# Boundary copies of turned blocks: from ScalarE out of PSUM to GpSimd out of SBUF, with another order of the turns

## The chip, the cores and the metric

The kernel runs on one core of a Trainium2 chip. The core has five engines that the profile names: PE (TensorE, matmuls; PEld is its loading of weights), DVE (VectorE), ACT (ScalarE), POOL (GpSimd) and SP (SyncE, which only issues DMAs here). Each engine works through its own instructions in a fixed order and waits for others through semaphores. The metric is the device time of one execution in microseconds (us), lower is better. Data is float32 throughout.

## The reference

The input x is 4 images of 256 channels and 64 x 64 pixels. Layer 0 computes a 7x7 convolution with dilation 2 to 128 channels, a 1x1 convolution to 49 channels, and a softmax over these 49; the result is used as per-pixel weights of the 49 shifted copies of x:

```
k = conv(x, w1, padding 6, dilation 2) + b1          # 4 x 128 x 64 x 64
k = conv1x1(k, w2) + b2                              # 4 x  49 x 64 x 64
attn = softmax(k, axis=1)
y[b,c,h,w] = sum over u,v of xpad[b,c,h+2u,w+2v] * attn[b,7u+v,h,w]
```

Layer 1 whitens y: it takes the mean and the 64 x 64 covariance of each of the 4 groups of 64 channels over all pixels, finds an inverse square root of it by five Newton steps, applies it to the centred y, and scales and shifts each channel.

## The kernel before, in words

The two convolutions are folded into one from 256 to 49 channels, computed in a transformed domain (evaluations of rows and columns at a few points, products on PE, interpolation back). The matmuls of this are in `conv_bank` (line 599, tile `cv`), one step for each image and row point, in three banks. DVE makes their inputs (`col_ops`, tile `xh`, lines 347, 350 and 354, with ScalarE copies at 541 and 547) and interpolates their results (tiles `pv`, `zz`, `lgx`, the same helper lines). ScalarE brings the products out of PSUM (line 610).

Dilation 2 splits an image into four phases; two of them share a slot of x in SBUF. Attention works through 16 phases of columns and rows, n = 0 to 15, four for each image. For each n the logits go through `softmax`, `move_terms` copies the weights into a skewed layout (tile `zt`) and POOL's DMA queue writes them to a scratch in DRAM (tile `sd`, line 1093); `load_band` reads them back through SP's DMA queue as a banded matrix (tiles `band` and `bandz`). The weighted sum over shifts is then a matmul of blocks of x with bands.

For that, a block of 8 x 16 pixels has to stand on the partitions. `make_block` (line 1162) turns it: two PE transposes (line 1169), one for each 128 channels, into a PSUM tile `tp`, and a copy of 128 x 256 into the SBUF tile `xb` (line 1175). There are three PSUM buffers of `tp`, which are also used by `turn_y` and `softmax`, and four buffers of `xb`. The phase is cut into an upper and a lower half of rows; each half has four blocks, `PIECES` (line 1188), and a fifth piece ("z"), the rows of the other half that the shifts reach at the boundary. This fifth piece is put together from half blocks: when the block with t8 = 1 or 2 is turned, 64 of its 128 partitions are copied a second time, to the upper or lower 64 partitions of the tile `xbz` (line 1183). ScalarE makes these copies, out of PSUM, like those to `xb`; once the list `tail` is filled, after the last conv step, DVE makes both.

`weighted_sum(n, half, k)` (line 1194, matmuls at 1211) adds piece k to the sum of the half, k = 4 or k = 0 being the boundary piece: the upper half ends with it, the lower half begins with it. The upper half's boundary piece comes from blocks of the lower half (t8 = 2), so these must be turned before the upper half is complete. `store_y` (1231 and 1229) brings the sum out of PSUM and adds a pivot. `turn_y` turns the result y back, for `moments` (line 1263), which sums the covariance in PSUM (tile `sig`).

`first_half(n)` and `second_half(n)` write these calls down; PE keeps program order. `first_half(n)` also turns the last four blocks of y of the phase before (`turn(4)` to `turn(7)`, line 1242) where that is still open. On the other engines the order is chosen by a scheduler with a cost model that gives the copies a high priority. `gap` puts a half after every few conv steps: the halves of n = 0 to 9 lie between conv steps (190 to 561 us), those of 10 to 15 follow the last conv step (561 to 662 us). After that `whiten` and the output stage follow.

POOL has almost no arithmetic: memsets at the start, and one pair of small copies (line 1424). Its queue issues the DMAs of lines 147, 161, 1093 and 1281.

Of the kernel before, what the change touches and what calls it, by code (L numbers as in the profile page):

```python
# [32 lines left out]
def kernel(  # L33
# [29 lines left out]
    nc = tc.nc  # L63
    B, C, H, W = x.shape
# [33 lines left out]
    def pe(ins):  # L98
        return tc.keep_in_program_order(ins)
# [9 lines left out]
    def tp():  # L109
        return ps_tp.tile([P, 512], F32, tag="tp", name="tp")  # L110
# [72 lines left out]
    t = tp()  # L183
# [3 lines left out]
    t = tp()  # L187
# [5 lines left out]
    for k in range(2):  # L193
        t = ps_cv.tile([P, 512], F32, name=f"cv{k}")
# [53 lines left out]
    for k, c0 in enumerate(range(0, P, CB)):  # L248
        n = min(CB, P - c0)
        t = cv_buf[k % 2]  # L250
# [15 lines left out]
    for k0 in range(0, KT, TB):  # L266
        n = min(TB, KT - k0)
        t = tp()
# [848 lines left out]
    def load_band(n, half):  # L1117

        if (n, half) in loaded or n not in moved:
            return  # L1120
        loaded.add((n, half))
        D = sd[n % 2][:]
        base = lambda t, h: (
            h * HS + TR8 * t * RS + (ROW0[t] - TR8 * t + R) * WS + COLS[h][0] - h * TC + R
        )
        t0 = 2 * half
        for h in range(2):
            nc.sync.dma_start(
                band[:, t0 : t0 + 2, h].rearrange("p t r w -> p t (r w)"),
                bass.AP(  # L1130
                    tensor=D.tensor,
                    offset=D.offset + base(t0, h),
                    ap=[[LS - 1, P], [base(t0 + 1, h) - base(t0, h), 2], [1, TROWS * WS]],
                ),
            )
        e = CR * half + (R if half else 0)
        for h in range(2):
            c0, c1 = COLS[h]
            dma = nc.sync.dma_start(
                bandz[h * 64 : (h + 1) * 64, half, :, c0:c1],  # L1140
                bass.AP(
                    tensor=D.tensor,
                    offset=D.offset + h * HS + (HALF - CR * half) * RS + e * WS + c0 - h * TC + R,
                    ap=[[LS - 1, 64], [WS, R], [1, c1 - c0]],
                ),
            )
        if (n, half) == (4 * B - 1, 1):
            bring_back(dma)

    blocks = {}  # L1150

    tail = []

    def tile_of(t, cc, t8, h, pc):

        return halves(t)[:, cc, h, TR8 * t8 : TR8 * (t8 + 1), bass.ds(pc, TC, 2)]

    def where(n):

        return slots[n // 2], n % 2  # L1160

    def make_block(n, m):

        xt, pc = where(n)
        t8, h = m
        t = tp()
        for cc in range(NCC):
            pe(
                nc.tensor.transpose(  # L1169
                    t[:, cc * P : (cc + 1) * P], tile_of(xt, cc, t8, h, pc), ident  # L1170
                )
            )
        xb = bpool.tile([P, C], F32, tag="xb", name=f"xb_{n}_{t8}{h}", bufs=4)
        with tc.high_priority():
            (nc.vector.tensor_copy if tail else nc.scalar.copy)(xb, t[:, :C])  # L1175
        blocks[n, m] = xb
        if t8 in (1, 2):
            z = ("z", 2 - t8)
            if h == 0:
                blocks[n, z] = bpool.tile([P, C], F32, tag=f"xbz{t8}", name=f"xbz_{n}_{t8}")  # L1180
            i = slice(0, 64) if t8 == 2 else slice(64, P)
            with tc.high_priority():
                (nc.vector.tensor_copy if tail else nc.scalar.copy)(  # L1183
                    blocks[n, z][h * 64 : (h + 1) * 64], t[i, :C]
                )


    PIECES = (
        ((0, 0), (0, 1), (1, 0), (1, 1), ("z", 0)),
        (("z", 1), (2, 0), (2, 1), (3, 0), (3, 1)),  # L1190
    )
    y_ps = {}

    def weighted_sum(n, half, k):

        m = PIECES[half][k]
        if k == 0:
            y_ps[n, half] = ps_y.tile([P, NCC, HALF, SW], F32, tag="y", name=f"y_{n}_{half}")
        ps = y_ps[n, half]
        xb = blocks[n, m]  # L1200
        if m[0] == "z":
            q0, nq = (HALF - R, R) if half == 0 else (0, R)
            c0, c1 = 0, SW
            rhs = bandz[:, half].rearrange("p r w -> p (r w)")
        else:
            q0, nq = ROW0[m[0]] - HALF * half, TROWS
            c0, c1 = COLS[m[1]]
            rhs = band[:, m[0], m[1], :, : c1 - c0]
        for cc in range(NCC):
            pe(  # L1210
                nc.tensor.matmul(  # L1211
                    ps[:, cc, q0 : q0 + nq, c0:c1],
                    xb[:, cc * P : (cc + 1) * P],
                    rhs,
                    start=(k == 0),
                    stop=(k == len(PIECES[half]) - 1),
                    skip_group_check=True,
                )
            )

    def store_y(n, half):
        yt, pc = where(n)
        ps = y_ps.pop((n, half))
        for cc in range(NCC):
            o = halves(yt)[:, cc, :, half * HALF : (half + 1) * HALF, bass.ds(pc, TC, 2)]
            i = ps[:, cc].rearrange("p r (h c) -> p h r c", h=2)
            with tc.high_priority():
                if tail and cc:
                    nc.vector.tensor_scalar(o, i, pivot[:, cc : cc + 1], None, ALU.add)  # L1229
                else:  # L1230
                    last = nc.scalar.activation(o, i, AF.Identity, bias=pivot[:, cc : cc + 1])  # L1231
        return last
# [4 lines left out]
    def turn_y(n, i):  # L1237
        yt, pc = where(n)
        t = tp()
        for cc in range(NCC):  # L1240
            pe(
                nc.tensor.transpose(  # L1242
                    t[:, cc * P : (cc + 1) * P],
                    tile_of(yt, cc, i // 2, i % 2, pc),
                    ident,
                )
            )
        yb = ybs[n, i] = yt_buf[i % NY]
        with tc.high_priority():
            return nc.scalar.copy(  # L1250
                yb.rearrange("p a g c -> p (a g) c")[:, :, :GW],
                t[:, :C].rearrange("p (e c) -> p e c", c=GW),
            )

    def moments(n, half):


        for i in range(4 * half, 4 * half + 4):
            yb = ybs.pop((n, i))
            for cc in range(NCC):  # L1260
                for g in range(P // GW):
                    pe(
                        nc.tensor.matmul(  # L1263
                            sig[g * GW : (g + 1) * GW, cc],
                            yb[:, cc, g, :GW],
                            yb[:, cc, g],
                            start=(count[0] == 0 and cc == 0),
                            stop=(count[0] == 4 * B * NCH - 1),
                            skip_group_check=True,
                        )  # L1270
                    )
            count[0] += 1
# [3 lines left out]
    def move(k):  # L1276

        nxt_k = {0: 5, 1: 6, 2: 7}.get(k)
        if nxt_k is not None:
            spill[k] = dram.tile([P, NCC * SH * W], F32, name=f"spill{k}")  # L1280
            nc.gpsimd.dma_start(spill[k], slots[k].rearrange("p a r w -> p (a r w)"))
            load_x(k, nxt_k, nc.gpsimd)
# [14 lines left out]
    def first_half(n):  # L1297
        last = open_n.pop() if open_n else None

        def turn(i):  # L1300
            if last is not None:
                turn_y(last, i)

        for m in PIECES[0][:2]:
            if (n, m) not in blocks:
                make_block(n, m)
        turn(4)
        turn(5)
        weighted_sum(n, 0, 0)
        make_block(n, PIECES[0][2])  # L1310
        turn(6)
        weighted_sum(n, 0, 1)
        make_block(n, PIECES[0][3])
        turn(7)
        make_block(n, PIECES[1][1])
        weighted_sum(n, 0, 2)
        make_block(n, PIECES[1][2])
        weighted_sum(n, 0, 3)
        weighted_sum(n, 0, 4)
        move_terms(n + 1, store_y(n, 0))  # L1320
        half_done.add(n)
        load_band(n + 1, 0)
        if last is not None:
            moments(last, 1)
            if last % 2:
                move(last // 2)
        make_block(n, PIECES[1][3])
        make_block(n, PIECES[1][4])
# [228 lines left out]
    n = [0]  # L1557
# [97 lines left out]
```

## Time and profile before

| | us |
|---|---|
| median of 3 runs | 741.35 (739.52 to 743.1) |
| the profiled execution | 735.81 |
| its span, first to last instruction | 734.0 |
| PE busy | 684.0 (93%) |
| DVE busy | 598.0 (81%) |
| ACT busy | 328.8 (45%) |
| POOL busy | 133.2 (18%), nearly all of it issuing DMAs |
| the 40 ACT copies to `xbz` | 368 ns each (median) |
| the 24 DVE copies to `xbz` | 422 ns each (median) |
| the 82 ACT copies to `xb` | 373 ns each (median) |

The stages, read from the profile: weights and the first image's conv steps up to about 190 us; conv steps of the other images with the attention of n = 0 to 9 between them up to 561; the rest of the attention up to 662; whitening up to 677; the output stage to the end. A row of the timeline gives start and duration in us, engine, line and operation, the tiles as out<-in, the shapes and, in brackets, how long the engine was idle before it and what ended that. "Busy" of PE is modelled and includes matmuls that overlap.

### The profile page before, as it was taken

The page shows a single profiled execution, that of the slowest core. Times are in us where ns is not written, and L with a number is a line of the kernel's source. Part 1 is how long each engine was busy: PE and PEld are TensorE (multiplying, and loading weights), DVE is VectorE, ACT ScalarE, POOL GpSimd, SP SyncE. Part 2 cuts the span into 40 slices and gives each one's busy share as a digit, 9 for nine tenths or more (in the row PEclk, how much of TensorE's full clock was granted, in tenths as well). Part 3 has the DMA queues.
Part 4 walks back from the last instruction along what each step waited for, and adds up shares of the span by engine and source line. Part 5 has one row for each costly group of instructions (what it writes and reads, how often), then busy time and mean ns, then how long its engine had stood idle before and what let it go on. Part 6 is the DMA issues. An engine that isn't in the chain of part 4 may idle for free.

```text
span 734.0 us, 19103 instructions
## 1 busy us (share of the span) xinstructions
PE 684.0 (93%) x7728; PEld 539.1 (73%) x7728; DVE 598.0 (81%) x1291; ACT 328.8 (45%) x919; POOL 133.2 (18%) x194
## 2 busy tenths in 40 slices
PE   6999999999898999998999999998999689997996
PEld 1449543478898988897999989888998678885231
DVE  3799998995796899999886899899998885435575
ACT  1424320133654655675545445716546222332564
POOL 0002526663021020020220200200211322100000
PEclk9999999999999999999999999999999979997899
DMA  8923999973665582157645820452641535472687
GB/s 322 259 92 103 239 387 212 229 179 90 169 173 150 206 299 68 60 188 257 173 111 201 266 69 1 104 168 72 166 103 37 106 75 126 107 271 117 246 354 316
DMA packets 78337, 126.10 MB, mean 172 GB/s; under 512 B 36471, under 2 KB 58664, under 8 KB 77096
## 3 DMA queue, kind: packets, MB, share of 16 engines
q1 hardware_dynamic: 59912, 64.52, 26.9%
q0 software_dynamic: 12288, 42.08, 21.8%
q10 hardware_dynamic: 6048, 18.27, 8.0%
q8 instruction: 61, 1.00, 0.5%
q14 instruction: 28, 0.23, 0.1%
HBM read 78.78 MB, written 52.36 MB: 179 GB/s over the span
## 4 chain that ended last, share of the span: by engine, by line
PE 38%; DVE 27%; issue 9%; ACT 6%; DMA 4%; POOL 4%; ACTq 0%; SPq 0%; POOLq 0%; DVEq 0%
PE cv L599 15%; PE y L1211 7%; PE tp L1595 4%; DVE xh L354 3%; PE tp L1242 3%; DMA band<-sd 3%; DVE pv L354 3%; POOL ahead L147 3%; PE sig L1263 3%; DVE zz L354 2%; PE tp L1169 2%; DVE rb L347 2%; DVE rb L354 2%; ACT d L1017 1%; DVE pv L350 1%
## 5 line engine op out<-in xcount | busy, mean ns | idle before, releaser
L599 PE MATMUL cv<-xh,wr 128*49 128x128 f32 x4160 | 231.5, 273 | 3.5 <-ACT xh L547 3.3
L599 PEld LDWEIGHTS cv<-xh,wr 128*49 128x49 f32 x4160 | 226.3, 124 | 6.9 <-ACT xh L547 3.5
L1211 PE MATMUL y<-band,xb 128*128 128x209 f32 x512 | 113.4, 348 | 7.0 <-DMA band<-sd 5.9
L1093 POOL DMA_DIRECT2D sd<-zt x128 | 67.3, 532 | 234.1 <-ACT zt L1076 159.9
L1211 PEld LDWEIGHTS y<-band,xb 128*128 128x128 f32 x512 | 87.8, 195 | 8.9 <-DMA band<-sd 4.8
L610 ACT COPY pv<-cv 113x486 f32<-113x486 f32 (+2 forms) x60 | 26.1, 435 | 95.6 <-PE cv L599 90.5
L1250 ACT COPY yt<-tp 128x256 f32<-128x256 f32 x128 | 45.4, 378 | 50.3 <-PE tp L1242 49.2
L1242 PE MATMUL tp<-ident,slot 128*128 128x128 f32 x256 | 51.4, 298 | 9.0 <-ACT yt L1250 6.7
L354 DVE SCALAR_TENSOR_TENSOR pv<-pv 113x162 f32<-113x162 f32 x176 | 53.1, 322 | 3.3 <-ACT pv L610 2.6
L1242 PEld LDWEIGHTS tp<-ident,slot 128*128 128x128 f32 x256 | 41.1, 205 | 15.9 <-ACT yt L1250 7.8
L1169 PE MATMUL tp<-ident,slot 128*128 128x128 f32 x256 | 50.0, 300 | 2.7 <-DVE xbz L1183 1.4
L1231 ACT ACTIVATE slot<-y,pivot 128x512 f32<-128x512 f32 x52 | 36.1, 741 | 34.5 <-PE y L1211 34.4
L1169 PEld LDWEIGHTS tp<-ident,slot 128*128 128x128 f32 x256 | 40.9, 204 | 6.2 <-DVE xbz L1183 1.8
L147 POOL DMA_DIRECT2D slot<-in_x_dram x20 | 33.9, 1695 | 50.6 <-issue 46.2
L1076 ACT COPY zt<-d 32x112 f32<-32x112 f32 (+2 forms) x132 | 38.2, 290 | 7.3 <-DVE d L1035 5.4
L1263 PE MATMUL sig<-yt 128*64 128x65 f32 x1024 | 37.7, 228 | 0.0
L1263 PEld LDWEIGHTS sig<-yt 128*64 128x64 f32 x1024 | 33.2, 140 | 5.7 <-issue 4.3
L354 DVE SCALAR_TENSOR_TENSOR xh<-ct 128x512 f32<-128x512 f32 x40 | 26.7, 689 | 12.4 <-PE cv L599 12.3
L1017 ACT ACTIVATE d<-tp,mx 128x49 f32<-128x49 f32 x96 | 27.5, 337 | 19.8 <-DVE mx L1000 19.8
L764 PE MATMUL acc<-slot,tap 128*49 128x256 f32 (+7 forms) x224 | 34.8, 468 | 0.0
L1175 ACT COPY xb<-tp 128x256 f32<-128x256 f32 x82 | 28.5, 376 | 11.6 <-PE tp L1169 11.1
L1229 DVE TENSOR_SCALAR slot<-y,pivot 128x512 f32<-128x512 f32 x12 | 9.0, 751 | 27.2 <-ACT slot L1231 27.1
(239 smaller groups left out, 1117.3 us busy)
## 6 DMA issues: line engine op xcount, KB each, us to landing
out_dram<-out SPq DMA_DIRECT2D x32, 512.0 KB, 3.6
band<-sd SPq DMA_DIRECT2D x64, 242.0 KB, 3.3
slot<-in_x_dram POOLq DMA_DIRECT2D x20, 512.0 KB, 7.1
sd<-zt POOLq DMA_DIRECT2D x128, 77.0 KB, 3.1
wr<-gd ACTq DMA_DIRECT2D x14, 588.0 KB, 5.3
wr<-gd ACTq DMA_DIRECT2D x14, 490.0 KB, 4.3
ahead<-in_x_dram POOLq DMA_DIRECT2D x12, 512.0 KB, 7.3
spill<-slot POOLq DMA_DIRECT2D x3, 2048.0 KB, 7.2
```

What stands on the lines that cost most here:

```text
L147: queue.dma_start(o[:, cc, h], src[:, :, pr, h * SW : (h + 1) * SW])
L354: return in_turn(STT(o, a, f, b, ALU.mult, ALU.add))
L599: nc.tensor.matmul(o, wv[:, sc, sr, cc], xv[bc][:, h * NCC + cc], start=(j == 0), stop=(j == len(terms) - 1), skip_group_check=True,)
L1017: nc.scalar.activation(d[:, h, i], lt[i // NI][:, i % NI, h, :KT], AF.Exp, bias=mx[:, i, h : h + 1], accum_out=s[:, h, i : i + 1],)
L1076: ins = nc.scalar.copy(o, i)
L1093: nc.gpsimd.dma_start(bass.AP(tensor=D.tensor, offset=D.offset + h * HS + g * RS, ap=[[LS, TC], [CR * RS, NCH], [1, KS * WS]],), zt[p0 : p ...
L1169: nc.tensor.transpose(t[:, cc * P : (cc + 1) * P], tile_of(xt, cc, t8, h, pc), ident)
L1211: nc.tensor.matmul(ps[:, cc, q0 : q0 + nq, c0:c1], xb[:, cc * P : (cc + 1) * P], rhs, start=(k == 0), stop=(k == len(PIECES[half]) - 1), s ...
L1231: last = nc.scalar.activation(o, i, AF.Identity, bias=pivot[:, cc : cc + 1])
L1242: nc.tensor.transpose(t[:, cc * P : (cc + 1) * P], tile_of(yt, cc, i // 2, i % 2, pc), ident,)
L1250: return nc.scalar.copy(yb.rearrange("p a g c -> p (a g) c")[:, :, :GW], t[:, :C].rearrange("p (e c) -> p e c", c=GW),)
L1263: nc.tensor.matmul(sig[g * GW : (g + 1) * GW, cc], yb[:, cc, g, :GW], yb[:, cc, g], start=(count[0] == 0 and cc == 0), stop=(count[0] == 4 ...
```

## The change

Outside the tail, the copy of the 64 boundary partitions is no longer made by ScalarE out of PSUM but by GpSimd, out of the SBUF block `xb` that ScalarE has just written. It therefore waits for the `xb` copy, and the PSUM buffer has one reader less. In `first_half` the second block of the upper quarter row is turned before `turn(6)` and the second sum, the first block of the lower half before `turn(7)`, and the second one before the third sum instead of before the fourth. The order applies to all 16 phases, the engine only to those before the tail.

```
             i = slice(0, 64) if t8 == 2 else slice(64, P)
             with tc.high_priority():
-                (nc.vector.tensor_copy if tail else nc.scalar.copy)(
-                    blocks[n, z][h * 64 : (h + 1) * 64], t[i, :C]
-                )
+                if tail:
+                    nc.vector.tensor_copy(blocks[n, z][h * 64 : (h + 1) * 64], t[i, :C])
+                else:
+                    nc.gpsimd.tensor_copy(blocks[n, z][h * 64 : (h + 1) * 64], xb[i])
...
         turn(5)
         weighted_sum(n, 0, 0)
         make_block(n, PIECES[0][2])
+        make_block(n, PIECES[0][3])
         turn(6)
         weighted_sum(n, 0, 1)
-        make_block(n, PIECES[0][3])
+        make_block(n, PIECES[1][1])
         turn(7)
-        make_block(n, PIECES[1][1])
+        make_block(n, PIECES[1][2])
         weighted_sum(n, 0, 2)
-        make_block(n, PIECES[1][2])
         weighted_sum(n, 0, 3)
         weighted_sum(n, 0, 4)
```

## The prediction

> **What bounds the kernel now.** I read the page first, for the engines' shares, then busy time by stretches, then the tile that the change is about, then the order of time in one of the places it touches.
>
> ```profile
> span 734.0 us, 19103 instructions
> PE 684.0 (93%) x7728; PEld 539.1 (73%) x7728; DVE 598.0 (81%) x1291; ACT 328.8 (45%) x919; POOL 133.2 (18%) x194
> ```
>
> PE is the bound on average, with 50 us idle in all. The stretches (us from the start; then PE, PEld, DVE, ACT, POOL busy) say more:
>
> ```profile
> 223.00:232.00 9.00, 7.14 (x70) 6.13 (x67) 8.93 (x16) 6.65 (x18) 0.30 (x1) 1.00 0.60 192
> ...
> 442.00:449.00 7.00, 6.80 (x71) 6.29 (x69) 6.93 (x6) 5.53 (x15) 0.00 (x0) 1.00 0.00 0
> ...
> 470.00:502.00 32.00, 28.50 (x520) 28.05 (x517) 30.98 (x68) 10.76 (x49) 4.05 (x8) 1.00 0.52 143
> ...
> 540.00:548.00 8.00, 7.80 (x80) 6.98 (x78) 7.69 (x15) 6.32 (x17) 0.00 (x0) 1.00 0.13 34
> ```
>
> 223 to 232, 442 to 449 and 540 to 548 hold the first halves of n = 1, 7 and 9. DVE has no gap in them and POOL does nothing. From 470 to 502 DVE, not PE, is the bound. The boundary tile, and who waits for the ScalarE copies of it:
>
> ```profile
> L1183 ACT COPY xbz<-tp x40: 363/368/374, 192.7 to 545.1; 64x256 f32<-64x256 f32 x40
> L1183 DVE COPY xbz<-tp x24: 406/422/428, 564.0 to 652.8; 64x256 f32<-64x256 f32 x24
> ```
>
> and from the list of waits (us in total, times, longest):
>
> ```profile
> PE y L1211 <- ACT xbz L1183: 5.5, 8, 1.5
> ```
>
> So the change touches 40 copies, four in each of ten first halves (n = 0 to 9); 24 stay on DVE. The end of the half of n = 9, PE and ScalarE rows, then DVE:
>
> ```profile
> 543.50 0.87 PE L1211 MATMUL y<-band,xb 128*128 128x209 f32 x4
> 544.21 0.39 PE L1169 MATMUL tp<-ident,slot 128*128 128x128 f32 x2
> 544.44 0.87 PE L1211 MATMUL y<-band,xb 128*128 128x209 f32 x4
> 545.51 0.69 PE L1211 MATMUL y<-bandz,xbz 128*128 128x96 f32 x4 [0.20 <-ACT xbz L1183]
> ```
>
> ```profile
> 544.71 0.38 ACT L1175 COPY xb<-tp 128x256 f32<-128x256 f32 x1
> 545.10 0.36 ACT L1183 COPY xbz<-tp 64x256 f32<-64x256 f32 x1
> ```
>
> ```profile
> 543.67 0.76 DVE L350 TENSOR_TENSOR zz<-zz 113x576 f32<-113x576 f32 x1
> 544.47 0.76 DVE L347 TENSOR_TENSOR zz<-zz 113x576 f32<-113x576 f32 x1
> ```
>
> The last block is turned at 544.21, one sum (0.7 us) covers its two ScalarE copies, and the boundary sum starts 0.20 late. The same wait in n = 0 to 8 is 0.30, 0.78, 1.50, 0.71, 0, 0.99, 0.25, 0.20, 0.87: 5.8 us with n = 9. At n = 1 the third block also waits 1.09 for a PSUM buffer that a boundary copy holds. Lastly the place that resets PE, and the only copy POOL makes:
>
> ```profile
> 497.44 1.81 PE L599 MATMUL cv<-xh,wr 128*49 128x128 f32 x29 [3.27 <-ACT xh L547]
> ```
>
> ```profile
> L1424 POOL COPY swap<-ident 128x64 f32<-128x64 f32 x2 | 0.4, 236 | 27.8 <-DVE lgx L354 27.8
> ...
> L295 POOL MEMSET zeros<- 128x256 f32 x1 | 0.3, 311 | 0.0
> ```
>
> At 497.44 PE has waited 3.27 us; the row names ScalarE, but DVE's last two writes of xh end at 497.33 and 497.94, so DVE was late.
>
> **The sum's base.** The profiled execution took 735.81 (span 734.0 and 1.81 around it); the median of the runs is 741.35, 5.54 more. I sum against 735.81 and add 5.54.
>
> **Part 1a, ScalarE loses 40 copies.** 40 x 0.39 start to start = 15.6 us of an engine busy 45%; it counts only where PE waits. A PSUM buffer comes free one copy (0.39) sooner, which removes the 1.09 at n = 1.
>
> **Part 1b, the order in a half.** Today the second block of the upper quarter is turned after the second sum and the last block just before the fourth. Now the last block is turned before the third sum, with two sums (1.43 us) ahead of the boundary sum. At n = 9 its transposes come 0.7 earlier, its ScalarE copy ends about 4.15 us after the half's start (540.22) and the boundary sum is due at 5.09. Instructions and sums stay the same in number; no DMA is moved.
>
> **Part 1c, a POOL copy alone.** No row has 64x256. From the copy of 64 elements (236 ns) and the memsets' slope ((311-205)/128 = 0.83 ns an element), 192 more elements make 395 ns. If what the copy takes beyond a 64-element memset (236-145 = 91 ns) also grows by the element, it is 670. I take 0.50, between, because only one copy row exists; ends 0.40 and 0.67. Ahead of it I put 0.15 (DVE's lgx ends 563.62, POOL's swap starts 563.77), behind it 0.1. If nothing else is in its way the last copy ends at 4.15+0.15+0.50+0.1 = 4.9, inside 5.09. That cover is 0.2 us thin.
>
> **Part 1d, a POOL copy beside DVE.** In the ten halves DVE is busy 82 of 87 us with 178 instructions, nearly all with two SBUF inputs, and the new copies read SBUF too. The only POOL copy of this trace ran when DVE had no such instruction, so no row tells whether they go side by side. Bounds: none of it (below), or POOL and DVE taking turns, each waiting for the other's whole instruction. The gain needs complete independence, since the cover is 0.2 and DVE has no gap, so I take turns as the likelier. In turns four copies wait for half an instruction and then for three whole ones, of a mean length L read from the stretch (busy by count). The first copy is ready 2.1 us after the half's start (n = 5, 7, 8 and 9 alike), so the boundary sum waits 2.1+0.15+4x0.50+3.5L+0.1-5.05 = 3.5L-0.7. By stretch: n = 1 (L 0.56) 1.26, n = 3 (0.47) 0.95, n = 5 (0.49) 1.0, n = 7 (1.16) 3.4, n = 8 (0.36) 0.56, n = 9 (0.51) 1.1. The halves without turned outputs, from their own starts: n = 2 1.8, n = 6 1.4. At n = 0 and 4 PE waits for the band DMA at the second sum; two copies are done by then, which leaves 0.7 and 0. DVE loses 4x0.5 = 2.0 us a half. Behind the waiting boundary sum PE has the moments, two block turns and the next conv bank queued, and ScalarE's store of y waits for it.
>
> [...]
>
> **What reaches the end, in turns.** PE delay, after minus before: n = 0 +0.4; n = 1 1.26-0.78-1.09 = -0.6; n = 2 +0.3 (the conv bank at 271.42 had its input 1.70 before, and DVE's 2.0 takes that too); n = 3 +0.2; n = 4 and 5 0; n = 8 -0.3. n = 6 and 7 delay PE by 4.3, of which the 3.27 at 497 swallows most, but DVE is full from 412 to 497 and comes 8x0.5 = 4.0 later: +4.0. Elsewhere the conv's inputs lie 4 to 19 us ahead of PE, so DVE's loss is hidden by that lead; without it each half would cost 2.0. After n = 9 DVE runs without a gap to its first tail copy at 563.54, which PE needs: +2.0 (PE's own 0.9 lies inside). Sum +6.0.
>
> **Part 2, the tail.** Six halves keep DVE copies: waits of 0.2 to 0.4 at the boundary sum (2.1 in all) and 1.42 at one block. The eight copies of a half are 8x0.42 = 3.4 us of DVE in a row, so the new order starts the last pair only some 0.3 earlier: I take -1.5, between -3.5 (all gone) and +1.4 (a turned output waiting for a DVE-held buffer costs what that block's wait did).
>
> **POOL's queue.** Copies share it with DMA issues of 0.53 each in eights (4.3). Those end at 223.30 and 373.73, before the copies of n = 1 and 5 are ready (225.4, 374.5); one load is issued at 342.24 inside n = 4, worth 0.57. The boundary copies for the second half's first sum are due 7 us later or more, and the block buffers they read are reused only after the boundary sum: no cost, unless POOL falls behind by more than that sum's wait.
>
> **Forecast:** 735.81+6.0-1.5 = 740.3, plus 5.54: **746**. With copies of 0.40 the sum is +2.6-1.5, 742.5; with 0.67 it is +11.9-1.5, 751.8. With the tail's ends the forecast's own range is 740 to 755.
>
> **Rivals.** (1) *Side by side, faster.* No interference, copies of 0.5: 5.8+1.09 of waits go, less 0.45 (n = 6 and 7, swallowed at 497), and 1.5 of the tail: -7.9, **733**. For it: POOL is idle in all ten halves. Against: the cover of 0.2 and DVE without gaps. It decides if a copy stays under 0.7 us beside DVE. (2) *POOL gets no turn while DVE has work queued.* At n = 9 DVE has no gap for 10 us; one half of 10 and two of 3 more make +16: **757** or more. Against: it needs the next DVE instruction always to win. (3) *Copies behind DMA issues*: a set of eight landing ahead of a last copy costs 4.3; two sets, beside the case (1): **742**. Against: the times above. (4) *It does nothing*: the removed waits reappear behind other ScalarE work (0.66 us xh copies stand before the last copy in n = 5 and 8), **741**.
>
> **Chances.** Turns 0.53 (slower 0.38, within 0.5% 0.12, faster 0.03); side by side 0.28 (faster 0.26, same 0.02); no turn 0.10; DMA issues 0.04 (same); nothing 0.05 (same 0.03, slower 0.02). Half a per cent, 3.7 us, is about what a measurement tells from no change. Faster 0.29, same 0.21, slower 0.50. The range runs from just below the first rival, 731, to the second, 757.
>
> **What would show it.** Turns: POOL copies of 0.4 to 0.7 that start 0.5 to 2 us after their ScalarE copy, boundary sums waiting about 1 us for POOL (n = 7 most), the wait at 497 near 7 us, DVE rows longer in the ten halves. Side by side: those sums start without a wait and DVE's means stay. What would make me wrong: a copy that is much longer than 0.67, or the order of ScalarE and DVE work shifting in the softmax of the last batch (580 to 594, where PE waits 5.9 us for reasons outside the change).

## The result and the profile after

The changed kernel takes 768.74 us (median; 768.54 to 769.98), the kernel before, run beside it, 740.43. The ratio is 1.0385 [1.036, 1.0409]: slower by 28 us, where 746 was forecast and 757 was the end of the range. The profiled execution took 768.57, its span is 766.8 (before 734.0).

The page of the changed kernel: the span, the engines, and two of the costliest groups (busy time and mean ns of one, then the idle time ahead of them and what ended it):

```profile
span 766.8 us, 19122 instructions
PE 693.2 (90%) x7728; PEld 549.1 (72%) x7728; DVE 601.2 (78%) x1291; ACT 314.2 (41%) x879; POOL 192.8 (25%) x234
...
L1186 POOL COPY xbz<-xb 64x256 f32<-64x256 f32 x40 | 59.7, 1493 | 135.4 <-ACT xb L1175 133.9
...
L1212 PE MATMUL y<-bandz,xbz 128*128 128x96 f32 x128 | 22.0, 300 | 35.1 <-POOL xbz L1186 35.1
```

PE's idle time went from 50.0 to 73.6 us, its busy time from 684.0 to 693.2 for the same 7728 matmuls. The two add up to the 32.8 by which the span grew. (The medians differ by 28.3: the profiled execution of the kernel before, 735.81, lies 4.6 under the median there.) The list of waits (us in total, times, longest) has what ended the idle time:

```profile
PE y L1212 <- POOL xbz L1186: 35.1, 9, 11.2
...
PE cv L599 <- ACT xh L547: 1.9, 1, 1.9
```

The boundary sums wait 35.1 us where they waited 5.5; all other idle time of PE together fell by 6.0. The answer for the boundary tile shows why (ns least, median and most, first and last start):

```profile
L1186 POOL COPY xbz<-xb x40: 396/744/12550, 192.8 to 580.7; 64x256 f32<-64x256 f32 x40
```

One copy takes 0.40 us at best, 0.74 in the median and 12.55 at worst. The 40 together are busy for 59.7 us, where 40 x 0.40 would be 16; the other 44 us GpSimd stood inside its copies. The worst one belongs to the first half of n = 8. Its rows of the timeline, POOL, then PE, then DVE from the moment the copy is released (the DVE rows are cut to the first and the last few):

```profile
527.83 12.55 POOL L1186 COPY xbz<-xb 64x256 f32<-64x256 f32 x1 [29.14 <-ACT xb L1175]
```

```profile
529.02 1.58 PE L1212 MATMUL y<-band,xb 128*128 128x209 f32 x8
541.80 1.17 PE L1212 MATMUL y<-bandz,xbz 128*128 128x96 f32 x4 [11.20 <-POOL xbz L1186]
```

```profile
527.80 0.32 DVE L354 SCALAR_TENSOR_TENSOR pv<-pv 113x162 f32<-113x162 f32 x1
528.04 0.32 DVE L347 TENSOR_TENSOR pv<-pv 113x162 f32<-113x162 f32 x1
528.28 0.56 DVE L350 TENSOR_TENSOR pv<-pv 113x162 f32<-113x162 f32 x2
...
535.49 2.36 DVE L354 SCALAR_TENSOR_TENSOR rb<-slot 128x1024 f32<-128x1024 f32 x2
537.76 2.36 DVE L354 SCALAR_TENSOR_TENSOR rb<-rb,slot 128x1024 f32<-128x1024 f32 x2
548.91 0.69 DVE L354 SCALAR_TENSOR_TENSOR xh<-ct 128x512 f32<-128x512 f32 x1 [8.79 <-PE cv L599]
```

DVE runs its queue without a gap: each row starts some 0.08 us before the one ahead of it has ended (535.49 + 2.36 = 537.85, the next at 537.76). It ends at 540.12, and the copy ends 0.26 later, at 540.38; the other three copies of the half then take 0.40 each. The last row tells why DVE stopped: its next instruction needs a product of PE, and PE is waiting for the copy. GpSimd got its turn when DVE had run out of work.

The five copies beside which three or more DVE instructions ended, worked out from the trace's records, with the wait of that half's boundary sum:

```
half   copy starts   copy takes   DVE instructions that ended beside it   DVE then stops for   sum waits
n = 8     527.83       12.55                    27                             8.79             11.20
n = 4     346.46        9.71                    21                             8.99              4.53
n = 1     225.50        4.55                     7                             0.035             4.57
n = 2     271.14        3.00                     5                             0.035             3.82
n = 3     306.12        2.49                     3                             4.63              1.39
```

All five end 0.26 to 0.27 us after a DVE instruction with a gap behind it. A gap of 0.035 us is what the records show where a DVE instruction reads the result of the one just before. Where DVE does such a chain (tile `zz`, n = 2, 6 and 9), one copy gets in after each instruction, and takes 0.58 to 0.83 (0.40 where it comes just at a gap).

The sums behind such a wait are slower as well: the boundary sum's four matmuls take 1.17 after the four longest waits (4.53, 4.57, 4.79 and 11.20 us), at a granted clock of 0.50, and 0.69 after the other five (0.53 to 3.82), at 1.00. The granted clock is 0.95 in the stretch of the halves (190 to 600 us) where it was 1.00 (190 to 562 before), and 0.955 over the whole span against 0.977. That fits the 9.2 us more of PE's busy time.

### The profile page after: what moved, and what is told of

The parts are those of the page before. It is cut to its first block, busy times and chain, and to the rows that moved or that the text cites. A ratio compares the mean times of both kernels' runs of the same rounds, so it can differ in the third digit from the quotient of the medians.

```text
span 766.8 us, 19122 instructions
## 1 busy us (share of the span) xinstructions
PE 693.2 (90%) x7728; PEld 549.1 (72%) x7728; DVE 601.2 (78%) x1291; ACT 314.2 (41%) x879; POOL 192.8 (25%) x234
## 4 chain that ended last, share of the span: by engine, by line
PE 51%; DVE 15%; issue 8%; POOL 7%; ACT 4%; DMA 3%; SPq 0%; ACTq 0%; POOLq 0%; DVEq 0%
PE cv L599 20%; PE y L1212 10%; PE sig L1264 4%; PE tp L1596 4%; POOL xbz L1186 4%; PE tp L1243 4%; PE tp L1169 3%; PE cv L764 3%; POOL ahead L147 2%; DMA band<-sd 2%; DVE xh L354 2%; DVE d L1035 2%; PE apply L1612 1%; PE cv L1612 1%; DVE zz L354 1%
## 5 line engine op out<-in xcount | busy, mean ns | idle before, releaser
L599 PE MATMUL cv<-xh,wr 128*49 128x128 f32 x4160 | 235.3, 276 | 1.9 <-ACT xh L547 1.9
L599 PEld LDWEIGHTS cv<-xh,wr 128*49 128x49 f32 x4160 | 230.3, 126 | 5.9 <-ACT xh L547 2.1
L1212 PE MATMUL y<-band,xb 128*128 128x209 f32 x512 | 110.5, 348 | 5.8 <-DMA band<-sd 5.6
L1186 POOL COPY xbz<-xb 64x256 f32<-64x256 f32 x40 | 59.7, 1493 | 135.4 <-ACT xb L1175 133.9
L1212 PE MATMUL y<-bandz,xbz 128*128 128x96 f32 x128 | 22.0, 300 | 35.1 <-POOL xbz L1186 35.1
L1243 PEld LDWEIGHTS tp<-ident,slot 128*128 128x128 f32 x256 | 41.4, 204 | 9.6 <-issue 3.6
L1169 PEld LDWEIGHTS tp<-ident,slot 128*128 128x128 f32 x256 | 39.0, 206 | 12.5 <-issue 8.5
L1212 PEld LDWEIGHTS y<-bandz,xbz 128*128 128x128 f32 x128 | 19.4, 213 | 38.6 <-POOL xbz L1186 38.6
L1264 PE MATMUL sig<-yt 128*64 128x65 f32 x1024 | 40.7, 238 | 0.0
L1264 PEld LDWEIGHTS sig<-yt 128*64 128x64 f32 x1024 | 36.0, 150 | 6.1 <-issue 4.9
```

The source lines that it names most:

```text
L599: nc.tensor.matmul(o, wv[:, sc, sr, cc], xv[bc][:, h * NCC + cc], start=(j == 0), stop=(j == len(terms) - 1), skip_group_check=True,)
L1169: nc.tensor.transpose(t[:, cc * P : (cc + 1) * P], tile_of(xt, cc, t8, h, pc), ident)
L1186: nc.gpsimd.tensor_copy(blocks[n, z][h * 64 : (h + 1) * 64], xb[i])
L1212: nc.tensor.matmul(ps[:, cc, q0 : q0 + nq, c0:c1], xb[:, cc * P : (cc + 1) * P], rhs, start=(k == 0), stop=(k == len(PIECES[half]) - 1), s ...
L1243: nc.tensor.transpose(t[:, cc * P : (cc + 1) * P], tile_of(yt, cc, i // 2, i % 2, pc), ident,)
L1264: nc.tensor.matmul(sig[g * GW : (g + 1) * GW, cc], yb[:, cc, g, :GW], yb[:, cc, g], start=(count[0] == 0 and cc == 0), stop=(count[0] == 4 ...
```

## The experiments

The theory after the result: GpSimd's read of SBUF is kept out by DVE for whole runs of instructions, and the boundary sums wait for that. The rivals: the new order costs the time; the copy's size or GpSimd's slowness costs it; GpSimd's writes are in the way; ScalarE did something useful before. All edits are made to the changed kernel, but for the last three, which are made to the order alone.

| kernel | us | ratio to before |
|---|---|---|
| changed kernel | 768.74 | 1.0385 [1.036, 1.0409] |
| order alone, ScalarE copies | 730.40 | 0.9869 [0.9836, 0.9901] |
| GpSimd alone, order as before | 775.89 | 1.0485 [1.0432, 1.0538] |
| 16 of 256 columns | 767.87 | 1.0377 [1.0325, 1.0429] |
| GpSimd writes, doesn't read | 731.72 | 0.9888 [0.9839, 0.9938] |
| DVE waits for each copy | 765.90 | 1.0359 [1.0316, 1.0402] |
| half of the copies on GpSimd | 739.51 | 1.0006 [0.9983, 1.0028] |
| DVE copies | 760.71 | 1.0291 [1.0222, 1.036] |

### The two parts apart

The order alone:

```diff
-                    nc.gpsimd.tensor_copy(blocks[n, z][h * 64 : (h + 1) * 64], xb[i])
+                    nc.scalar.copy(blocks[n, z][h * 64 : (h + 1) * 64], t[i, :C])
```

> Only the new order; the boundary copies stay on ScalarE out of PSUM. Theory (GpSimd's copies get no turn while DVE's two-input instructions follow one another): without GpSimd the loss is gone, 733 to 741 us, and the boundary sums of the ten halves wait under 3 us in all (5.8 before). Rival (the order itself costs, through PSUM buffers and queues): 750 us or more.

GpSimd alone, with the calls of `first_half` in the order of the kernel before:

```diff
         make_block(n, PIECES[0][2])
-        make_block(n, PIECES[0][3])
         turn(6)
         weighted_sum(n, 0, 1)
-        make_block(n, PIECES[1][1])
+        make_block(n, PIECES[0][3])
         turn(7)
-        make_block(n, PIECES[1][2])
+        make_block(n, PIECES[1][1])
         weighted_sum(n, 0, 2)
+        make_block(n, PIECES[1][2])
         weighted_sum(n, 0, 3)
```

> Only the engine: GpSimd copies out of SBUF, the order of before. Theory: the last copy becomes ready 0.7 us nearer to the boundary sum, so each of ten halves may wait 0.7 us more: 765 to 780 us, sums waiting for GpSimd 33 to 45 us. Rival (the order costs): about 745 us.

Measured: 730.40 and 775.89. The order alone is faster than both kernels and a little better than expected. In its list of waits the 5.5 us of the boundary sums are down to this:

```profile
PE y L1211 <- ACT xbz L1183: 0.8, 2, 0.6
```

GpSimd alone has the long waits too, 31.0 us where 33 to 45 were expected:

```profile
PE y L1212 <- POOL xbz L1186: 31.0, 8, 11.2
```

So the whole loss is GpSimd's and the order gains 10 us. The changed kernel is 38 us above the order alone. Between these two profiles the boundary waits differ by 35.1 - 0.8 = 34.3 us; the idle time of PE as a whole by 28.2 (73.6 against 45.4), its busy time by 10.2 (693.2 against 683.0, at a granted clock of 0.955 against 0.979), which add up to the 38.4 between the spans. Between the profiles of the kernel before and of the order alone it is 5.6 (734.0 and 728.4), not 10: the granted clock of the executions is 0.968 to 0.977 before and 0.972 to 0.981 with the order alone, and whether the order is the cause of that difference stays open.

### What of the copy is held up

The copy cut to 16 columns. A memset of the whole half block comes ahead of it, so 240 of 256 channels of the boundary pieces are zeros:

```diff
-                    nc.gpsimd.tensor_copy(blocks[n, z][h * 64 : (h + 1) * 64], xb[i])
+                    zb = blocks[n, z][h * 64 : (h + 1) * 64]
+                    nc.gpsimd.memset(zb, 0.0)
+                    nc.gpsimd.tensor_copy(zb[:, :16], xb[i, :16])
```

> As the changed kernel, but GpSimd copies 16 of the 256 columns (the other columns of the boundary block are zeros from an earlier GpSimd memset, so the boundary sums are not those of the reference). Theory: what costs is the wait for a turn, not the copying; 755 to 770 us, the longest copy still over 5 us, waits for GpSimd 25 us or more. Rival (GpSimd is slow at copying 64x256): a sixteenth of the data, so 745 us or less and no copy over 1.5 us.

No reading at all; the boundary pieces before the tail are zeros:

```diff
-                    nc.gpsimd.tensor_copy(blocks[n, z][h * 64 : (h + 1) * 64], xb[i])
+                    nc.gpsimd.memset(blocks[n, z][h * 64 : (h + 1) * 64], 0.0)
```

> As the changed kernel, but GpSimd fills the boundary half blocks with zeros instead of copying (no read, and no wait for the block; the boundary sums are left without their data). Theory: only an instruction that reads SBUF is held up by DVE; 730 to 739 us, no fill over 0.6 us. Rival (DVE keeps GpSimd from SBUF altogether, or GpSimd's queue with its DMA issues is what is late): fills of several us, 750 us or more.

Measured: 767.87 and 731.72. The groups of the page, first the kernel with 16 columns, then the one that only writes:

```profile
L1188 POOL COPY xbz<-xb 64x16 f32<-64x16 f32 x40 | 49.6, 1240 | 120.1 <-ACT xb L1175 118.6
```

```profile
L1186 POOL MEMSET xbz<- 64x256 f32 x40 | 12.2, 307 | 218.9 <-PE y L1212 213.8 <-PE acc L764 4.3
```

A copy of a sixteenth of the size, 0.19 us where it is undisturbed, still takes 1.24 us in the mean and 12.35 at most, and the kernel gains nothing by it: the size made no difference here. A memset of the full size takes 0.307 us wherever it lies, about what the 128 x 256 memset took in the profile before (0.3 us), and 37 of the 38 us are gone. (The memset needs no block to be turned, so it can start earlier than a copy; but 31 of the 40 run wholly beside DVE instructions with two operands, at 0.305 to 0.312 us.) What DVE keeps out here is GpSimd's reading of SBUF (copies of up to 12.55 us), not its writing.

### Three ways around it

Here DVE is made to wait for each copy by a one-column copy that reads the boundary block:

```diff
                     nc.gpsimd.tensor_copy(blocks[n, z][h * 64 : (h + 1) * 64], xb[i])
+                    probe = work.tile([P, 1], F32, tag="probe", name=f"probe_{n}_{t8}{h}", bufs=2)
+                    nc.vector.tensor_copy(
+                        probe[h * 64 : (h + 1) * 64], blocks[n, z][h * 64 : (h + 1) * 64, :1]
+                    )
```

> As the changed kernel, but behind each GpSimd copy DVE gets a copy of one column of the boundary block, so that it has to stop until GpSimd has finished. Theory (GpSimd's copy needs a moment in which DVE's two-input instructions do not follow one another): the stop gives it that moment; the longest copy falls from 12.6 to under 3 us, sums waiting for GpSimd from 35 to under 12 us, time 735 to 750 us, which is what the prediction had for taking turns. Rival (the wait is GpSimd's own, whatever DVE does): 765 us or more.

Measured: 765.90, a miss; by its time alone the rival (765 or more) would fit. The scheduler put the readers late in DVE's order, so copies still took up to 9.6 us. But the long ones of three halves, followed in the records, ended just where a reader stopped DVE. In the half of n = 8, POOL (two copies in one row), then DVE:

```profile
529.47 6.93 POOL L1186 COPY xbz<-xb 64x256 f32<-64x256 f32 x2 [29.07 <-ACT xb L1175]
```

```profile
534.78 0.32 DVE L350 TENSOR_TENSOR pv<-pv 113x162 f32<-113x162 f32 x1
535.39 0.14 DVE L1188 COPY probe<-xbz 64x1 f32<-64x1 f32 x1 [0.29 <-POOL xbz L1186]
```

Eighteen instructions after the release DVE comes to the first reader. Its queue was not empty at 535.10, it was only made to wait, and the first copy, which had stood since 529.47, ended at 535.36. So GpSimd's wait is not its own: in these halves it ended where DVE stopped. That the remedy failed says nothing against the cause; it names what is needed, a stop of DVE at the right place.

Only half of the copies on GpSimd, those of t8 = 1, which are due later, for the second half's first sum:

```diff
+                elif t8 == 2:
+                    nc.scalar.copy(blocks[n, z][h * 64 : (h + 1) * 64], t[i, :C])
                 else:
                     nc.gpsimd.tensor_copy(blocks[n, z][h * 64 : (h + 1) * 64], xb[i])
```

> New order; GpSimd copies only the two half blocks that the second half needs (t8 = 1), ScalarE the two that end the first half. Theory: the late copies are no longer in front of the boundary sum, so PE does not wait for GpSimd there; but the block buffer that a late copy reads is needed again for the third block after it, which in the two longest cases (10 and 12 us) holds up ScalarE: 731 to 742 us. Rival (any GpSimd copy costs what its wait costs, about 0.9 us each): 748 us or more.

Measured: 739.51, no change from before and 9 worse than the order alone. The boundary sums wait for GpSimd no more (one waits 1.6 for ScalarE), but the copies still stand (up to 16.03 us) and hold the blocks that they read:

```profile
ACT xb L1175 <- POOL xbz L1188: 16.0, 5, 11.1
...
PE cv L599 <- ACT pv L615: 9.1, 1, 9.1
```

ScalarE waits for one of the four `xb` buffers, and PE, once, for ScalarE's work queued behind that. A copy that nobody needs for 7 us still costs, if it stands longer than its source is free to stay.

DVE makes all boundary copies, as in the tail:

```diff
-                if tail:
+                if True:
```

> New order; DVE makes all boundary copies, out of PSUM. Each half gives DVE 4 x 0.42 us more, as much as GpSimd's turns were to cost it in the prediction. If DVE's lead over PE hides that except at the wait at 497 us and at the tail, as the prediction had it, the time lies 3 to 7 us above the new order alone: 733 to 738 us. If DVE is the bound in most stretches: 745 us or more.

Measured: 760.71, a miss by 22. The copies queue in DVE's order, and until they are done they hold the PSUM buffers that the next transposes need:

```profile
PE tp L1169 <- DVE xbz L1184: 20.0, 6, 7.1
...
PE tp L1243 <- DVE xbz L1184: 10.9, 4, 4.1
```

Of the three engines tried for these copies ScalarE serves best: 730.40 against 760.71 with DVE and 768.74 with GpSimd.

### When DVE gives a turn

The last three kernels add groups behind the end of the work: DVE instructions in a row, with GpSimd copies of 64 x 256 released beside them by a DVE copy (line 1658, 1666 or 1664; in two groups of the last kernel by ScalarE), so their total times say nothing. The first one, ten instructions of 128 x 512 of five kinds, one after another in program order:

```diff
...
+    for j, kind in enumerate((two, one_psum, psum_only, one, reduce)):
+        s, g = qs[j % 2][:, :256], qg[j % 2][:, :256]
+        keep(nc.vector.tensor_copy(s, chain[0]))
+        keep(nc.gpsimd.tensor_copy(g[0:64], s[64:128]))
+        keep(nc.gpsimd.tensor_copy(g[64:128], s[0:64]))
+        for k in range(10):
+            keep(kind(k))
+        chain[0] = g
```

> The kernel with the new order alone, and behind its end five groups: DVE makes a block, GpSimd copies its halves (two copies of 64x256) while DVE runs ten instructions of one kind on 128x512: sum of two SBUF operands; sum of one SBUF and one PSUM operand; copy out of PSUM; multiple of one SBUF operand; reduction of one SBUF operand. Theory: GpSimd's first copy ends under 0.8 us after its block with all kinds that read SBUF once, and only after the tenth instruction (6 us or more) with two SBUF operands. Rival (any busy DVE keeps GpSimd out): late in all five. Rival (GpSimd is late for its own reasons): late in none. The additions lengthen the kernel by some 30 us, which says nothing.

Measured, the first GpSimd copy of each group, in the order: two operands in SBUF, one in SBUF and one in PSUM, a copy out of PSUM, one SBUF operand times a constant, a reduction:

```profile
724.59 0.73 POOL L1659 COPY qg<-qs 64x256 f32<-64x256 f32 x1 [102.68 <-DMA out_dram<-out]
...
731.15 0.40 POOL L1659 COPY qg<-qs 64x256 f32<-64x256 f32 x1 [5.02 <-DVE qs L1658]
...
737.33 0.40 POOL L1659 COPY qg<-qs 64x256 f32<-64x256 f32 x1 [5.34 <-DVE qs L1658]
...
743.51 3.55 POOL L1659 COPY qg<-qs 64x256 f32<-64x256 f32 x1 [5.33 <-DVE qs L1658]
...
747.91 0.40 POOL L1659 COPY qg<-qs 64x256 f32<-64x256 f32 x1 [0.39 <-DVE qs L1658]
```

Beside additions with an operand in PSUM, copies out of PSUM and reductions GpSimd's copies took 0.40 us, as long as the shortest in the kernel. The products with a constant, which ran at 0.34 us each, half the time of the others, kept it out to the end of all ten. But the additions of two SBUF operands, the kernel's main kind, let it in by turns here. Both are against what was expected of them. So the kind alone doesn't say why it stands for 27 instructions in the kernel. The second one asks whether multiply-and-add, length or the moment makes the difference:

```diff
...
+    for j, (kind, lead) in enumerate(
+        ((stt, 0), (tt, 4), (mixed, 4), (small, 4), (long, 2), (in_place, 4))
+    ):
+        s, g = qs[j % 2][:, :256], qg[j % 2][:, :256]
+        for k in range(lead):
+            keep(kind(k))
+        keep(nc.vector.tensor_copy(s, chain[0]))
...
```

> ScalarE's copies out of PSUM with the new order, and behind the end of the kernel's work six groups, each with a DVE copy that releases two dependent-free GpSimd copies of 64x256 and then ten DVE instructions of one kind, all with two SBUF operands: multiply-and-add of 128x512; addition of 128x512 with four more of them ahead of the release; the two kinds in turn; addition of 113x162; multiply-and-add of 128x1024; addition of 128x512 in place, each on the result of the one before. The total time says nothing (25 to 35 us of added work). Theory, that the kind of instruction decides: the additions let a GpSimd copy in after one instruction, as the ten additions of before did (copies of 0.73 and 0.75), and the multiply-and-adds keep it out for several, so the first copy beside them takes over 2 us (128x512) and over 3 us (128x1024). Rival, that it is the length or the moment and not the kind: then the copies beside the multiply-and-adds of 128x512 take 0.7 to 0.8 as well, and those beside the short or the long ones differ. Only the chain in place has a pause after every instruction, in which both expect a turn.

Measured, the first copy of the first, second and fourth group:

```profile
726.19 0.73 POOL L1667 COPY qg<-qs 64x256 f32<-64x256 f32 x1 [103.06 <-DVE qs L1666]
...
735.16 8.62 POOL L1667 COPY qg<-qs 64x256 f32<-64x256 f32 x1 [7.43 <-DVE qs L1666]
...
752.18 2.57 POOL L1667 COPY qg<-qs 64x256 f32<-64x256 f32 x1 [5.98 <-DVE qs L1666]
```

My theory on the kind fell. Multiply-and-adds gave turns (0.73). The same additions of 128 x 512 that gave turns before now kept a copy out for 8.62 us: ten of them and the four instructions of the next group, until DVE itself had to wait. What changed is what ran ahead of the release: memsets and a copy there, here four additions, behind the ten multiply-and-adds of the first group without a gap. The short ones, with four ahead in the same way, kept it out for all ten (2.57). In the third and sixth group DVE had a pause just ahead, or one after each instruction, and the copies took 0.80. The long ones gave turns as well (1.33), but all ten wrote the same tile, so each had to wait for the one before; that group doesn't test length.

The third one varies what lies ahead of the release. Additions of 128 x 512 in all groups, none, or four of them, ahead of the release, and ten behind it (in the last group those behind it have one operand in PSUM):

```diff
...
+    for kind, lead, how, copies in (
+        (tt, 0, "DVE", 6),
+        (tt, 0, "late", 2),
+        (tt, 4, "PSUM", 2),
+        (tt, 4, "ACT", 2),
+        (tt, 4, "DVE", 2),
+        (one_psum, 4, "DVE", 2),
+    ):
...
```

> ScalarE's copies out of PSUM with the new order, and behind the end six groups of ten DVE additions of 128x512 with two SBUF operands (the last group: one operand in PSUM), none on the result of the one just before it, with GpSimd copies of 64x256 released beside them. Every group begins with a pause of DVE. (1) released right after the pause, six copies; (2) released after the pause by a chain of six ScalarE copies, some 2 us later; (3) to (5) released after four additions without a pause, by a DVE copy out of PSUM, by a ScalarE copy, by a DVE copy out of SBUF; (6) like (5), the additions behind it with one operand in PSUM. The total time says nothing. [...] Rival, that the DVE copy out of SBUF right before decides and not the pause: (2), (3) and (4) show turns as (1) does, and (5) alone a long copy.

The theory that this tests: DVE gives turns only shortly after a pause (copies of 0.73 to 0.8 us in group 1), and a copy released later stands until DVE stops (4 us or more in groups 2 to 5); in group 6 a copy takes about 0.4.

Measured, one row for each group (the copies of a group in one row):

```profile
725.72 4.75 POOL L1671 COPY qg<-qs 64x256 f32<-64x256 f32 x6 [102.86 <-DVE qs L1664]
736.00 3.95 POOL L1671 COPY qg<-qs 64x256 f32<-64x256 f32 x2 [5.54 <-ACT qs L1668]
743.15 1.53 POOL L1671 COPY qg<-qs 64x256 f32<-64x256 f32 x2 [3.20 <-DVE qs L1664]
752.60 6.18 POOL L1671 COPY qg<-qs 64x256 f32<-64x256 f32 x2 [7.92 <-ACT qs L1662]
761.85 6.60 POOL L1671 COPY qg<-qs 64x256 f32<-64x256 f32 x2 [3.07 <-DVE qs L1664]
771.52 0.85 POOL L1671 COPY qg<-qs 64x256 f32<-64x256 f32 x2 [3.07 <-DVE qs L1664]
```

Groups 1, 4, 5 and 6 went as the theory had it, and group 2 too but for the size (its first copy took 3.50, where 4 or more were expected). The copy released in the first addition after other work (here memsets) got its turn, and so did the five behind it: 4.75 / 6 = 0.79 each. The copies released nearly three microseconds into the run of additions, or after four or five of them, stood until DVE stopped, whether ScalarE or a DVE copy from SBUF released them (3.95, 6.18 and 6.60 for the two copies of a group). Group 3 corrects the theory: turns came without a pause. A DVE instruction that reads PSUM, put between the fourth and the fifth addition, was enough for turns (0.77 each). So what sets these groups apart is whether DVE had been reading two SBUF operands for several instructions without a break when the copy was released. The kernel has one copy that doesn't fit: at n = 0 one was released at 196.14, while the fourth such instruction of 113 x 162 without a gap was running, and had its turn after that one and the next (0.60).

## Why the prediction was wrong

**Parts 1a and 1b, right in size; the credit went to the wrong part.** The first rival priced the change without interference at -7.9, 733. With nothing read by GpSimd it is 731.72, and the order with ScalarE's copies reaches 730.40. So freeing ScalarE of 40 copies, part 1a, shows no gain of its own; the order made all of it.

**Part 1c, the copy alone: its lower end was right.** 0.40 us measured (0.396 at best in the kernel), taken as 0.50, the ends 0.40 and 0.67.

**Part 1d is the step that failed.** It said that no row tells whether the two engines go side by side, and set the bounds at "none of it" and "taking turns". The upper bound was no bound: nothing in the trace said that a turn must come after one DVE instruction. So the wait was priced by the mean length of a DVE instruction, where the runs show that it goes by how long DVE runs on without a gap. By turns the ten sums were to wait 12 us in all; they waited 35.1. Where DVE does chains the turns are there and the formula is near (n = 6: 1.63 against 1.4; n = 7, with instructions of 2.3 us: 4.79 against 3.4). Where DVE runs free it is far off (n = 8: 11.20 against 0.56; n = 4: 4.53 against 0; n = 1: 4.57 against 1.26). The table of the five long copies and the last two experiments put this down to how DVE's run stood when the copy was released. n = 8 was to be the cheapest of the halves with turned outputs, as its instructions are the shortest; its row of the stretches before shows DVE busy for 9.00 of 9.00 us, with 25 instructions:

```profile
502.00:511.00 9.00, 8.13 (x89) 7.39 (x84) 9.00 (x25) 6.55 (x18) 0.00 (x0) 1.00 0.23 69
```

And n = 9, read as a half without a gap, has gaps that the prediction's own rows show: 543.67 + 0.76 = 544.43, and the next row starts at 544.47. Its sum waited 0.53, where 1.1 was forecast.

That a waiting copy gets in after one whole DVE instruction was the author's estimate, and no row before shows it. The runs show it in the chains (0.58 to 0.83 us a copy) and not at n = 8, where the copy was passed by 25 DVE instructions that started after it (12.55 us). Beside DVE instructions with two SBUF operands GpSimd's reading was held up and its writing was not (memsets of 0.307 us).

**DVE's loss, put too high.** It was to lose 4 x 0.5 us in every half and so make PE late at 497 (near 7 us). DVE, which nearly always went first, lost little: it is busy 601.2 us against 598.0, 3.2 more in all, and the wait at that place is 1.9. The forecast's +6.0 was in sum what DVE was to lose (4.0 at 497, 2.0 behind n = 9), the engine that hardly pays. Nor did the wait of 3.27 at 497 swallow most of what n = 6 and 7 cost PE: their sums waited 6.42 us for GpSimd instead of 0.45 for ScalarE, and the wait there fell by 1.4 only, since DVE now had to wait for PE (four waits of 1.05 to 2.79 us from 472 to 496).

**The second rival was the mechanism**, with a chance of 0.10 and a price of +16. Against it stood that "it needs the next DVE instruction always to win". Once a run of instructions was under way it did here, but for the copy at 196.14. Its price took 10 us for n = 9 and 3 each for two more halves. That one wait came out near 10 (11.20) is luck: it is that of n = 8, and n = 9 waited 0.53. n = 1, 2, 4 and 7 cost 3.8 to 4.8 each, and the slower clock behind the waits wasn't in the sum at all: 9.2 us more of PE's busy time.

**Part 2 and POOL's queue, nearly right.** The waits of the six tail sums (2.1 us) and of one block (1.4) are gone from the list; the wait for an output turn of 5.9 came back as two of 7.7 in all for boundary copies. That is -1.7 net, where -1.5 was forecast; the order alone shows the same 7.7, so nothing of the 38 lies there. The copies don't hold up the DMA issues in GpSimd's queue to any cost: waits for the bands are 5.6 us in all against 5.9. The other way round, one issue of 0.53 to 0.57 stands ahead of the last copy in n = 1, 4, 5 and 9, where one in n = 4 was forecast: at most 2.2 of the 35.1 us.

## What to carry to other kernels

Before a copy on the critical path moves to an idle engine, look at what it will read there, and what the busy engines read at the time: here ScalarE out of PSUM was safe (0.363 to 0.374 us in all 40 copies before), and GpSimd out of SBUF, 0.40 alone, took up to 12.55 beside a DVE that ran without a gap. Where the trace has no row for a contention, "by turns" isn't its upper bound; take as the bound the longest stretch in which the other engine runs without a break, and put it on every place where that can happen. And try the two halves of a change apart: the reordering alone was worth 10 us of the median (ratio 0.9869) and was buried under the 38 of the other half.

## What the hardware showed that was not expected

- In the added groups a GpSimd copy that was released in the first two-operand instruction after memsets (0.73 us), a pause (0.80) or an instruction that reads PSUM (0.77) had its turn after one DVE instruction, and six in a row did (0.79 each). The same copy released after four such instructions without a break waited for all that followed (8.62 us past fourteen). In the kernel, 21 of the 27 copies of over 0.45 us ended at a DVE gap of 0.034 us or more; the other six had waited for one or two instructions only. Why a run, once it stands, isn't interrupted, and why the copy at 196.14 came in all the same, stays open; the profile has no record of what a copy waits for once it has started.
- Products of an SBUF operand with a constant, at 0.34 us each, kept GpSimd out for all ten (3.55 us) though ten reads of PSUM and only one copy in SBUF lay ahead of them. Additions behind a read of PSUM gave turns (0.77), so this kind differs; whether always, one group doesn't tell.
- DVE hardly paid. In turns with a copy, two additions took 0.88 us each instead of 0.68; in the kernel its busy time grew by 3.2 us while GpSimd stood for 44.
- The boundary sums behind the four longest waits (4.53 to 11.20 us) were slower: the same four matmuls took 1.17 us instead of 0.69, at a granted clock of 0.50 instead of 1.00. Why the clock was lower there, no trace shows.
